# First group's value products taken pair by pair into four open banks, and router products placed between the steps of the maxima

## The chip, the cores and the metric

The kernel runs on one core of one Trainium2 chip. A core has TensorE (matrix products, PE in the profile), VectorE (DVE), ScalarE (ACT), GpSimd (POOL) and SyncE (SP, which here only issues DMAs), and 16 DMA engines that serve the queues of SP, ScalarE and GpSimd. Engines run side by side and wait for one another by semaphores; each works through its own queue in order. The metric is the device time of one execution in microseconds (us); lower is better. All data are 32-bit floats.

## The reference

`x` is 4096 x 512, the context `ctxt` is 3202 x 512. The first half of the layer is a gated attention of the rows of `x` over the context:

```python
encoder_hc = layernorm(x)                       # 4096 x 512
Sim  = (encoder_hc @ w1)[:, None] + (ctxt @ w2)[None, :] + (encoder_hc * w3) @ ctxt.T + b
A    = softmax(Sim, axis=context)
hq   = A @ ctxt                                 # the "values" product
Batt = softmax(max(Sim, axis=context), axis=rows)
hc   = Batt @ encoder_hc
hcq  = concat([encoder_hc, hq, encoder_hc * hq, encoder_hc * hc]) @ W_qv + b_qv
x    = x + tanh(g_xattn) * hcq
```

The second half is a mixture of 8 experts with 2 choices per row: router logits `layernorm(x) @ w_router`, capacity 640 rows per expert, `gelu(rows @ w1 + b1) @ w2 + b2`, and a gated sum back into the rows.

## The kernel before

**Tiling.** The 4096 rows are worked in 8 groups of 512. The context is cut into two halves of 12 tiles of 128 rows; tile j of both halves makes a pair (`NJ` = 12 pairs), and one tile of 128 and two single rows are left over. `PAIRS` joins two pairs at a time, so a group's score stage has six steps. Most products are done in Strassen's manner: seven products of quarter blocks in place of eight, with sums of the blocks formed on VectorE.

**Stages of a group g.** `stage_s(g)` makes the scores: in each of the six steps seven products (`pas`, `p6s`, `p7s`, `pbs`, `pas` again, `p4s`, `pbs` again; L507), each of eight TensorE instructions, and VectorE's sums of them (L467 to L481), of which L474 reads `pbs` between its two products; then the scores of the left-over tile (`sc`, L531), running maxima `M` (L525), a transposition (`mps`, L546), a reduction, and a product that spreads the maxima along rows (`mbps`, L159). `stage_d(g - 1)` makes the output products of the group before (L820). `stage_e(g)` subtracts the maxima on VectorE (L579) and takes exponentials on ScalarE (L580); VectorE sums them (L588). `stage_v(g)` makes the values product (`product`, L639). In it `between()` prepares the queries of the next group (`stage_w`, `stage_a` with L343 to L348 and the sums L189 to L192), and `early()` loads them. `stage_n(g)` reads rows of a later group for their means and variances and for single columns (L312 to L323, L183). At the end of `stage_v`, the two left-over context rows are added (L734), row sums (`rsps`, L738) give the scale `ri`, and the left operand of the output products is formed (L750 to L768).

**The first group is different.** It builds for the later groups what they only load. `build` forms the sums of the transposed context (`ktb`) and stores them (`kt_d`, L515). In `stage_v(0)` the values are not in Strassen's manner: in four passes (two column halves of 256, and in each the two context halves), value tiles of 6 x 128 x 256 are loaded by `load_values` (L442, L448) and multiplied into two open banks. Beside that, VectorE builds the sums of the values (`build_values`, L387 to L390), from row tiles that `rows_of_pair` loads separately (L380), into tiles `vs` with two buffers, which GpSimd's queue stores in `vs_d` (L391). It also builds the weights of the output products from `W_qv` (`build_weights`, L411 to L423), stored in `wt_d`. `router_weights` loads all of `W_qv` transposed (`wq`, L281), and 64 small products (L289, 8 columns wide) multiply it with the router's weights; one goes behind each value product (`beside`). Their result is copied to `we` (L664, L678, L679), which `build_weights` needs.

**What sets the order.** The program is traced once; a scheduler orders each engine's queue by program order among what it takes to be ready, with its own idea of durations. `tc.issue_after(ins)` puts what its block traces on the engine of `ins` behind `ins` in that queue. The list `queue` holds loads on SP's queue, and `queue[-1]` the latest of them. Tiles of one tag share buffers: tag `st` has five (keys, value tiles, output weights), `vs` two, `vc` two. There are six PSUM banks for products (`bank`) and two for transpositions (`ps_tr`).

Of the kernel before, what the change touches and what calls it, by code (L numbers as in the profile page):

```python
# [20 lines left out]
def gated_layer(ctx, tc, x, x_t, ctxt, ctxt_t, ctxt_c, ctxt_r, g_xattn, g_ffn, w_sim, w_sim_r, b_sim, W_qv, W_qv_t, b_qv, b_qv_c, w_router, b_router, w1, b1, w2, b2, out):  # L21
# [102 lines left out]
    with ExitStack() as s1:  # L124
# [141 lines left out]
        def router_weights():  # L266
# [16 lines left out]
            def products(ps, ks):  # L283

                for k in ks:
                    for a, f0, n in parts[k]:
                        for f in range(n // P):
                            for d in range(DC):
                                nc.tensor.matmul(  # L289
# [4 lines left out]
                                yield  # L294
# [3 lines left out]
        def we_bank(name):  # L298
            return bank(name).rearrange("p a b -> p (a b)")[:, : 4 * DC * E].rearrange("p (k c e) -> p k c e", k=4, c=DC)
# [76 lines left out]
        def rows_of_pair(j, name):  # L376
            vc = sb.tile([P, 2, D], F32, name=f"vc{name}{j}", tag="vc", bufs=2)
            for h in range(2):
                with tc.issue_after(queue[-1].ins):
                    nc.sync.dma_start(vc[:, h, :], ctxt[h * LH + j * P : h * LH + j * P + P, :])  # L380
            return vc

        def left_sums(name, vc, dst):
# [6 lines left out]
            tt(vs[:, 3, :], A12, vs[:, 1, :], ALU.subtract)  # L390
            nc.gpsimd.dma_start(dst, vs)  # L391

        def build_values(j):

            left_sums(f"v{j}", rows_of_pair(j, "v"), vs_d[j // JH][:, :, j % JH, :])

        def build_rest_values():
            vc = sb.tile([P, 2, D], F32, name="vcr", tag="vc", bufs=2)[:, 0, :]
            with tc.issue_after(queue[-1].ins):
                nc.sync.dma_start(vc, ctxt[LC : LC + P, :])  # L400
            vd = sb.tile([P, 256], F32, name="vd", tag="vs", bufs=2)
            tt(vd, vc[:, :256], vc[:, 256:], ALU.subtract)
            nc.gpsimd.dma_start(vd_d, vd)
# [79 lines left out]
        def stage_s(g):  # L483
# [8 lines left out]
            for jj, js in enumerate(PAIRS):  # L492
# [23 lines left out]
                if g == 0 and jj == 2:  # L516
                    with tc.issue_after(e_add.ins):
                        stage_a_rest(first_qs)
                if jj == 4 and 0 < g < NG - 1:
                    ahead[g + 1] = stage_n(g + 1)  # L520
# [7 lines left out]
            for i, terms in enumerate((((0, "1"), (1, "2")), ((2, "3"), (3, "7")))):  # L528
                for a, p in terms:
                    for k in range(2):  # L530
                        nc.tensor.matmul(  # L531
# [9 lines left out]
            tt(M[:, :, 0, :], M[:, :, 0, :], ec, ALU.max)  # L541
            if g == 0:
                live[g]["we"] = router_weights()
            ps = ps_tr.tile([P, 4, P], F32, name=f"mps{g}", tag="tr")
            for i in range(4):
                tr = nc.tensor.transpose(ps[:, i, :], M[:, i // 2, 0, (i % 2) * P : (i % 2 + 1) * P], ident)  # L546
# [4 lines left out]
            diag_rows(ps, f"m{g}", mt)  # L551
# [17 lines left out]
        def stage_e(g, first):  # L569
# [26 lines left out]
            if first:  # L596
                for h in range(2):
                    for jj in range(n_jj):
# [25 lines left out]
        def stage_v(g, early, between):  # L624
# [8 lines left out]
            def product(ps, what, right, start=True, stop=True, rest=None, right_c=None, beside=iter(())):  # L633
                for i in range(2):
                    vt = load_values(g, what, i, rest)
                    js = list(range(i * JH, (i + 1) * JH)) + ([NJ] if i and rest is not None else [])
                    for j in js:
                        for b in range(2):
                            mm = nc.tensor.matmul(  # L639
                                ps[b], vt[:, j - i * JH, b * P : (b + 1) * P], right(j) if j < NJ else right_c,  # L640
                                start=start and j == 0 and (b == 0 or g == 0), stop=stop and i == 1 and j == js[-1],
                                skip_group_check=True,
                            )
                            with tc.issue_after(mm.ins):
                                next(beside, None)
                return mm

            if g == 0:
                ps12, ps03 = we_bank("we12"), we_bank("we03")
                w12, w03 = v["we"](ps12, [1, 2]), v["we"](ps03, [0, 3])  # L650
                for i in range(2):
                    ps = [bank(f"vv{i}_{b}") for b in range(2)]
                    for h in range(2):
                        product(
                            ps, (h, i * 256), lambda j: E[j // 2][:, :, h, j % 2, :], start=h == 0, stop=h == 1,
                            rest=rest_of(i * 256) if h else None, right_c=ec, beside=w03 if i else w12,
                        )
                        if (i, h) == (0, 0):
# [839 lines left out]
```

## Time and profile before

| | |
|---|---|
| median of 3 runs | 2675.95 us (2674.36 to 2680.94) |
| the profiled execution's own time | 2675.19 us |
| its span in the trace | 2673.4 us |
| mean granted clock of TensorE | 0.988 |
| first group's `sc`, start in the trace | 90.56 us |
| first value product (`vv`) | 102.09 us |
| `rsps` of the first group | 204.64 us |
| second group's `sc`, start | 305.66 us |

The span is what the trace covers; the execution's own time is 1.8 us longer. Times inside the span count from its start. Two TensorE records make one 32-bit product. "L474" is line 474 of the kernel before. An arrow in brackets names what ended an idle stretch.

### The profile page before, as it was taken

What the parts mean: (1) busy time and instruction counts of PE and PEld (TensorE: products, weight loads), DVE (VectorE), ACT (ScalarE), POOL (GpSimd) and SP (SyncE); (2) the same over time, 40 slices, a digit from 0 to 9 for tenths busy, and PEclk for the clock granted to TensorE, in tenths of its full rate; (3) what the DMA queues carried; (4) which work ended last, traced back from release to release, by engine and by line L of the source; (5) the groups of instructions that cost most, each with busy time, mean ns of one, the idle gap of its engine ahead of it and who ended that gap; (6) DMA issues with size and microseconds to landing.
All of it is one profiled execution on the core that took longest, in us unless ns stands there. A gap on an engine that the chain in (4) does not pass through costs nothing. (4 is left out here: it accounts for less than half of the span.)

```text
span 2673.4 us, 29708 instructions
## 1 busy us (share of the span) xinstructions
PE 2593.4 (97%) x11200; PEld 2096.8 (78%) x11200; DVE 1706.4 (64%) x3432; ACT 458.4 (17%) x788; POOL 241.7 (9%) x301
## 2 busy tenths in 40 slices
PE   8996999999999999999999996999999999999998
PEld 7655888888888888888888875777777777777776
DVE  7854766856947768569466556574747575565654
ACT  1200110200201102002011143211121211111111
POOL 0110000100000001000000056000101010101010
PEclk9998999999999999999999997999999999999999
DMA  7776674756746747567446694322313242323210
GB/s 274 253 237 220 178 250 172 198 196 184 243 153 177 252 162 201 204 178 240 162 146 208 230 357 148 131 107 89 123 67 126 76 145 83 107 87 103 75 60 20
DMA packets 185007, 442.62 MB, mean 166 GB/s; under 512 B 17806, under 2 KB 84750, under 8 KB 182816
## 3 DMA queue, kind: packets, MB, share of 16 engines
q1 hardware_dynamic: 156960, 358.81, 41.1%
q0 software_dynamic: 17872, 51.46, 5.6%
q10 hardware_dynamic: 10032, 30.46, 2.9%
q8 instruction: 88, 1.44, 0.2%
q14 instruction: 55, 0.45, 0.1%
HBM read 362.27 MB, written 85.55 MB: 168 GB/s over the span
## 5 line engine op out<-in xcount | busy, mean ns | idle before, releaser
L507 PE MATMUL pas<-Qp,kt 128*128 128x256 f32 x672 | 161.6, 382 | 0.0
L1246 PE MATMUL pah<-bT,w 128*128 128x320 f32 x512 | 159.3, 434 | 0.5 <-ACT p1h L1253 0.5
L639 PE MATMUL pbv<-E,vt 128*128 128x256 f32 x672 | 147.3, 379 | 0.0
L507 PEld LDWEIGHTS pas<-Qp,kt 128*128 128x128 f32 x672 | 128.0, 191 | 17.4
L639 PEld LDWEIGHTS pbv<-E,vt 128*128 128x128 f32 x672 | 127.7, 190 | 17.4
L1246 PEld LDWEIGHTS pah<-bT,w 128*128 128x128 f32 x512 | 97.5, 191 | 39.8 <-ACT p1h L1253 1.0
L580 ACT ACTIVATE E<-E 128x1024 f32<-128x1024 f32 x96 | 100.9, 1057 | 129.5 <-DVE E L579 128.6
L579 DVE TENSOR_TENSOR E<-E,mb 128x1024 f32<-128x1024 f32 x96 | 115.3, 1216 | 11.4 <-ACT mb L566 11.4
L1246 PE MATMUL pao<-w,h 128*128 128x256 f32 x512 | 120.9, 379 | 0.0
L1429 POOL DMA_INDIRECT out<-acc,ti x40 | 40.9, 1022 | 863.0 <-DVE dc L1295 529.0
L1017 PE MATMUL x1p<-W,q2T 128*128 128x264 f32 x512 | 117.4, 390 | 0.0
L1406 PE MATMUL op<-w,h 128*128 128x512 f32 x256 | 114.8, 592 | 0.0
L1246 PEld LDWEIGHTS pao<-w,h 128*128 128x128 f32 x512 | 97.3, 190 | 20.1 <-issue 7.7
L1017 PEld LDWEIGHTS x1p<-W,q2T 128*128 128x128 f32 x512 | 97.7, 192 | 16.5
L463 ACT COPY p1s<-pas 128x512 f32<-128x512 f32 x48 | 28.1, 586 | 464.5 <-issue 257.2
L507 PE MATMUL pbs<-Qp,kt 128*128 128x256 f32 x336 | 81.3, 386 | 21.4 <-DVE E L474 21.4
L525 DVE TENSOR_TENSOR M<-M,E 128x1024 f32<-128x1024 f32 x80 | 97.9, 1224 | 4.5
L507 PEld LDWEIGHTS pbs<-Qp,kt 128*128 128x128 f32 x336 | 64.8, 193 | 30.8 <-DVE E L474 21.8
L1406 PEld LDWEIGHTS op<-w,h 128*128 128x128 f32 x256 | 46.6, 190 | 48.7 <-issue 41.4
L507 PE MATMUL pbs<-q,kt 128*128 128x256 f32 x336 | 79.4, 379 | 2.9 <-DVE we L679 2.9
L479 DVE TENSOR_TENSOR E<-p4s,u3s 128x512 f32<-128x512 f32 x48 | 33.1, 689 | 75.4 <-PE p4s L507 75.4
L1368 DVE TENSOR_TENSOR h<-p4h,u3h 128x320 f32<-128x320 f32 x64 | 31.3, 489 | 78.1 <-PE p4h L1246 78.1
(467 smaller groups left out, 5423.1 us busy)
## 6 DMA issues: line engine op xcount, KB each, us to landing
kt<-kt_d SPq DMA_DIRECT2D x84, 896.0 KB
w<-in_w SPq DMA_DIRECT2D x32, 2048.0 KB
vt<-vs_d SPq DMA_DIRECT2D x56, 768.0 KB
wp<-wt_d SPq DMA_DIRECT2D x56, 520.0 KB
kt_d<-ktb ACTq DMA_DIRECT2D x12, 896.0 KB
buf_d<-zero SPq DMA_DIRECT2D x80, 129.0 KB
xb<-buf_d SPq DMA_DIRECT2D x40, 258.0 KB
r<-r_d SPq DMA_DIRECT2D x32, 260.0 KB
```

The source lines that it names most:

```text
L463: nc.scalar.copy(p1, pa)
L479: tt(done(1, 0), p4, u3, ALU.add)
L507: nc.tensor.matmul(ps[:, jl, :], kts[j][:, KSLOT[p], k, :], B[p][:, k, :], start=start and jl == 0 and k == 0, stop=stop and k == 1, skip_ ...
L525: tt(M, M, e[:, :, h], ALU.max)
L579: live[g]["last"] = tt(e, e, m, ALU.subtract)
L580: live[g]["exp"] = nc.scalar.activation(e, e, AF.Exp)
L639: mm = nc.tensor.matmul(ps[b], vt[:, j - i * JH, b * P : (b + 1) * P], right(j) if j < NJ else right_c, start=start and j == 0 and (b == 0 ...
L1017: mm = nc.tensor.matmul(ps[:, j, :B1], qTs[g][:, c, q * P : (q + 1) * P], W1[:, c, j, :], start=(c == 0), stop=(c == DC - 1))
L1246: nc.tensor.matmul(ps, a, b, start=start and i == 0, stop=stop and i == len(A) - 1, skip_group_check=True)
L1368: tt(hi[:, :HC], ps, u, ALU.add)
L1406: nc.tensor.matmul(ps, hT[:, k, 2 * MH :], W2[:, k, :], start=(k == 0), stop=(k == KH - 1))
L1429: sc = nc.gpsimd.indirect_dma_start(out=out[:, :], out_offset=rows_of(ti, s), in_=acc[:, :], in_offset=None, bounds_check=N - 1, oob_is_er ...
```

## The change

1. *Values of the first group.* One pass over the pairs in place of four. `rows_of_pair(j)` loads both tiles of pair j in one DMA of 512 KB into a buffer of tag `st`, the loads being members of `queue`. TensorE takes the left operands of four products per tile from it, into four open banks, and VectorE's sums of the values read the same buffer. The separate value loads go. The scaled queries of the second group come behind the sums of the ninth pair (`sums`).
2. *Exponentials of the first group* are taken step by step with both context halves, in place of one half after the other.
3. *Router products.* The weights are loaded from the fourth step of the first group's scores on. All 64 products go into one bank, in a fixed order: 12 behind `sc`, 12 behind the transposition, 24 behind `mbps`, and one behind each of the first 16 value products, those of the first two pairs.
4. *Moved into the second group's scores:* behind the last sum (`e_add`) of step 0 the rest rows and `rsps` (`rest_rows`), behind that of step 1 the left operand (`left_operand`), and behind those of steps 1 to 4 one `build_weights` each. In the other groups `rest_rows` and `left_operand` stay at the end of `stage_v`.

```diff
+        def behind(mm, products, n):
+            for _ in range(n):
+                with tc.issue_after(mm.ins):
+                    mm = next(products, mm)
+            return mm
...
+        def rows_of_pair(j):
+            vc = st.tile([P, 2, D], F32, name=f"vc{j}", tag="st")
+            with tc.issue_after(queue[-1].ins):
+                if j < NJ:
+                    rows = ctxt[:LC, :].rearrange("(h j p) d -> p h j d", h=2, p=P)[:, :, j, :]
+                    queue.append(nc.sync.dma_start(vc, rows))
+                else:
+                    queue.append(nc.sync.dma_start(vc[:, 0, :], ctxt[LC : LC + P, :]))
             return vc
...
                 if g == 0 and jj == 2:
                     with tc.issue_after(e_add.ins):
                         stage_a_rest(first_qs)
+                if g == 0 and jj == 3:
+                    live[g]["we"] = router_weights()
+                if g == 1:
+                    with tc.issue_after(e_add.ins):
+                        if live["then"]:
+                            live["then"].pop(0)()
+                        if 0 < jj <= DC:
+                            build_weights(jj - 1)
...
-            if g == 0:
-                live[g]["we"] = router_weights()
+                beside = live[g]["we"](pw, [1, 2, 0, 3])
+            mm = behind(mm, beside, 12)
             ps = ps_tr.tile([P, 4, P], F32, name=f"mps{g}", tag="tr")
             for i in range(4):
-                tr = nc.tensor.transpose(ps[:, i, :], M[:, i // 2, 0, (i % 2) * P : (i % 2 + 1) * P], ident)
+                with tc.issue_after(mm.ins):
+                    mm = nc.tensor.transpose(ps[:, i, :], M[:, i // 2, 0, (i % 2) * P : (i % 2 + 1) * P], ident)
+            mm = behind(mm, beside, 12)
...
-            diag_rows(ps, f"m{g}", mt)
+            with tc.issue_after(mm.ins):
+                mm = diag_rows(ps, f"m{g}", mt)
+            live[g]["beside"], live[g]["mm"] = beside, behind(mm, beside, 24)
...
-                for h in range(2):
-                    for jj in range(n_jj):
+                for jj in range(n_jj):
+                    for h in range(2):
                         powers(E_t[jj][:, :, h], mb.unsqueeze(2).to_broadcast([P, 2, 2, 256]))
...
+                ps = [bank(f"vv{b}") for b in range(DC)]
+                for j in range(NJ + 1):
+                    vc = rows_of_pair(j)
+                    for h in range(2 if j < NJ else 1):
+                        for b in range(DC):
+                            with tc.issue_after(mm.ins):
+                                mm = nc.tensor.matmul(
+                                    ps[b], vc[:, h, b * P : (b + 1) * P], E[j // 2][:, :, h, j % 2, :] if j < NJ else ec,
+                                    start=j == 0 and h == 0, stop=j == NJ, skip_group_check=True,
+                                )
+                            mm = behind(mm, beside, 1)
+                    with tc.issue_after(v["last"].ins):
+                        if j < NJ:
+                            total = build_values(j, vc)
+                        else:
+                            build_rest_values(vc[:, 0, :])
+                    if j == 2:
+                        with tc.issue_after(v["last"].ins):
+                            nc.vector.tensor_copy(we, v["pw"])
+                    if j == 3:
+                        with tc.issue_after(v["last"].ins):
+                            ahead[1] = stage_n(1)
+                    if j == 5:
+                        early()
+                    if j == 8:
+                        v["sums"] = total
+                for b in range(DC):
+                    nc.scalar.copy(hqT[:, b, :], ps[b].rearrange("p a b -> p (a b)"))
                 between()
...
+            if g:
+                rest_rows()
+                left_operand()
+            else:
+                live["then"] = [rest_rows, left_operand]
...
-                    stage_a(g + 1, live.pop("qT"), ahead[g + 1][0], live[g]["last"], live[g]["exp"])
+                    stage_a(g + 1, live.pop("qT"), ahead[g + 1][0], live[g].get("sums", live[g]["last"]), live[g]["exp"])
```

## The prediction

> **What bounds the kernel now.** First the page's busy times: TensorE is busy nearly throughout, so a change pays only where TensorE waits, works twice or works cold.
>
> ```profile
> PE 2593.4 (97%) x11200; PEld 2096.8 (78%) x11200; DVE 1706.4 (64%) x3432; ACT 458.4 (17%) x788; POOL 241.7 (9%) x301
> ```
>
> Second, the waits of TensorE from 0 to 260 us (us in total, times, longest). Nearly all the idle time that the diff can reach is one wait of 21.4 us at the second group's start.
>
> ```profile
> PE pbs L507 <- DVE E L474: 23.3, 3, 21.4
> ...
> PE vv L639 <- ACT E L580: 3.0, 1, 3.0
> PE pbs L507 <- DVE we L679: 2.9, 1, 2.9
> PE mbps L159 <- DVE dgm L158: 1.7, 1, 1.7
> PE mps L546 <- DVE M L541: 1.4, 1, 1.4
> ```
>
> Third, TensorE's timeline: start, length, instruction, idle before. A value product and a router product take 1.09 together (112.00 to 113.09), a value product alone 0.858 (24 instructions, two to a product, in 10.30, 142.56 to 152.86): the router's adds 0.22.
>
> ```profile
> 90.56 3.62 PE L531 MATMUL sc<-Qp,kcb 128*128 128x256 f32 x16
> ...
> 102.09 2.07 PE L639 MATMUL vv<-E,vt_(0_0)_0_821 128*128 128x512 f32 x2 [3.02 <-ACT E L580]
> ...
> 112.00 1.10 PE L639 MATMUL vv<-E,vt_(0_0)_0_821 128*128 128x512 f32 x2
> 112.95 0.28 PE L289 MATMUL we<-wrc,wq 128*128 128x8 f32 x2
> 113.09 1.10 PE L639 MATMUL vv<-E,vt_(0_0)_0_821 128*128 128x512 f32 x2
> ...
> 142.56 10.46 PE L639 MATMUL vv<-E,vt_(1_0)_1_977 128*128 128x512 f32 x24
> ...
> 204.64 0.95 PE L738 MATMUL rsps<-ones,mb 128*128 128x1 f32 x8
> ...
> 240.99 3.78 PE L507 MATMUL pbs<-Qp,kt 128*128 128x256 f32 x8 [21.38 <-DVE E L474]
> ```
>
> Fourth, VectorE's timeline just before 241. It stands still for store landings between the last sums, then takes the first group's rest rows and left operand, and only at 240.24 the sum that frees TensorE's bank. So it is VectorE's order, not its load, that stops TensorE.
>
> ```profile
> 225.01 0.42 DVE L402 TENSOR_TENSOR vd<-vcr 128x256 f32<-128x256 f32 x1 [2.82 <-DMA vs_d<-vsv]
> 228.49 0.43 DVE L419 TENSOR_TENSOR wt<-wc 128x260 f32<-128x260 f32 x1 [3.06 <-DMA vs_d<-vsv]
> ...
> 230.01 0.74 DVE L734 SCALAR_TENSOR_TENSOR hqT<-prb,cr,hqT 128x512 f32<-128x512 f32 x1
> ...
> 240.24 0.69 DVE L474 TENSOR_TENSOR E<-pbs,u3s 128x512 f32<-128x512 f32 x1
> ```
>
> **The change part by part.** Against the profiled execution's 2675.19 us, 0.8 below the median.
>
> *Stall removed.* Rest rows, left operand and right-hand weights go behind steps 0 to 4 of the second group's scores. 2.88 + 21.38 = 24.3 go. After the stall 14 matmuls took 5.97 (240.99 to 246.96) where the next eight took 1.72, 0.216 each: 14 x 0.216 = 3.0, so 2.9 of half clock go too.
>
> *Router products.* The stretch from the end of `sc` (94.18) to 204.64 is 110.5 now. After: 48 of the 64 products stand before the values. Alone, eight such small matmuls took 0.81 (204.64 to 205.45), so a product of two costs 0.20: 48 x 0.20 = 9.6, transposes 0.7, column product 0.9. Values start at 94.2 + 11.2 = 105.4, which is 3.3 later than now, since 9.6 of work goes into 6.1 of waits (1.4 + 1.7 + 3.0) and the order is strict: transposes and column product stand behind their 12 products even when their data is ready. Then 100 value products x 0.858 = 85.8 and 16 router products x 0.22 = 3.5: end 194.7. Gain 204.6 - 194.7 = 9.9, which includes 2.3 of half-clock start. `rsps` (0.8) only moves. Four bank copies of 0.59 on ScalarE now follow the last value where two did; the second group's third product is the first to need one of these banks, 3.5 in, so 0.
>
> *Their weights,* eight loads of 512 KB on SP's queue, are issued from the fourth step of the first group's scores on. A window query gives a DMA share of 0.00 for 60 to 65, and SP waits there for a key buffer, so I take 0; if they came as late as now (issued until 89.9, used at 103), the maxima would wait up to 9.
>
> *Rows shared.* Thirteen row loads replace ten value loads and 25 row loads; 6.4 MB less traffic. TensorE takes 8 x 0.858 = 6.9 per pair (8.6 in the first two); five buffers let loading run 34 us ahead. What is new is that a buffer is freed only when VectorE's four sums (4 x 0.34 = 1.4) are done too. VectorE's queue in this phase: 15 of subtraction, 15 of column sums, 13 of `stage_n`, 19 of sums, 10 of query work and pooling: 72 in the 95 from 100 to 195. I take 0: the lead of 34 hides it, and rival 3 is what it costs without that cover. Two waits are added on VectorE. The copy of the router weights needs the 64th product, at 105.4 + 16 x 1.08 = 123; VectorE is busy with column sums until then, and the sums of values behind the copy have their lead: 0. The query work of the second group now stands behind the ninth pair's sums, at about 160, and takes some 10 with ScalarE's four scalings; ScalarE and then TensorE's second group wait for it, and that group starts at 195: 25 to spare. The new order of the exponentials delivers two pairs per 2.3 against a use of 13.8: 0.
>
> *Work moved.* Rest rows 8 x 0.66 + 4 x 0.61 + 0.9 = 8.6; left operand 4 x 1.14 + 4 x 0.61 + 0.1 = 7.1; weights 1.5 each. A step of the scores is 7 x 1.727 = 12.1 on TensorE with 5.7 on VectorE. The last of a step's seven products goes into `pbs` again and so needs E (L474) done 10.4 after the step's start, while the moved work enters behind the last add of the step before. In step 1: that add 0.7, rest rows 8.6, one maximum 1.1, then u2, u3 and E 1.9: 12.3, about 2 too many; step 2, with left operand and first weights (8.6 again), the same. Later steps get 1.5 more each, the last of them beside the 11 of `stage_n` that it has now without a stall. A new stall of 4.2, between 0 (if the planner interleaves as at 60 to 80 us, with VectorE full and 0.2 lost) and 10. On SP's queue the key loads stand behind the weight loads; they run a step ahead (12), and a landing costs 3 to 6, so 0. GpSimd gets eight weight stores, and the last two decide when the first group's output products start: VectorE is done about 68 after the group's start, issue 0.8, landing 5.5 (a store issued until 222.98 released VectorE at 228.49), weight load 3: 77, against keys 72.5, stall 4.2 and `sc` 3.5: 80. Cost 0, with a margin of 3; without it, rival 1.
>
> **Two rules against it.** GpSimd's rows under a busy VectorE:
>
> ```profile
> 107.73 6.41 POOL L563 TENSOR_SCALAR nl<-lmax 128x1 f32<-128x1 f32 x1 [9.00 <-issue]
> ...
> 164.57 0.71 POOL L391 DMA_DIRECT2D vs_d<-vsv  x1 [9.77 <-DVE vsv L390]
> ```
>
> The first took 6.41 while VectorE ran its subtractions without a gap (the same instruction of the second group, among sums from PSUM, took 0.36 at 321.48); the store issue took 0.71 though VectorE ran gapless there too. The Trainium skill ("SBUF — State Buffer", "SBUF: two separate sides") says that VectorE and GpSimd share a port pair held by one of them for a whole instruction, and that GpSimd's DMA descriptors can be starved so. By the rule the stores lose up to the 8.6 of rest rows, output products start 5 late: 2648. By the store's row, nothing. I take the row, which is of the same kind of instruction.
>
> ```profile
> 98.00:100.00 2.00, 1.07 (x2) 0.24 (x2) 0.49 (x4) 0.59 (x1) 0.38 (x1) 1.00 1.07 388
> 100.00:102.00 2.00, 0.00 (x0) 0.00 (x0) 2.00 (x2) 1.02 (x1) 0.00 (x0) 0.50 1.04 383
> ```
>
> These are two rows of TensorE's windows; after the busy times come PEclk, the granted clock, then DMA share and GB/s. TensorE worked 1.07 of 2 and then nothing, and the clock was half from 100 until 107. The skill ("TensorE: Matmul & The Clock Gate", "What's actually happening") has the clock halved after an idle window of about 3.4 us and restored after a busy one. It does not say whether eight-column products count as busy. If not, the last 24 cost 0.40 each (+4.8) and the values start cold (+2.3): 7.1 worse. I take full clock, because with the products TensorE has no idle stretch left between 94 and 105; both ends are in the range.
>
> **Sum.** 24.3 + 2.9 + 9.9 = 37.1, less 4.2: 32.9. 2675.2 - 32.9 = 2642.3; on the median 2643.
>
> **Rivals.**
> 1. The work moved stops the second group (0.21): GpSimd's queue is in order, and `stage_n` of the third group waits there for a landing (12.0 at L322 in this group now); weight stores behind it start the output products some 9 late, or VectorE waits inside the steps for store landings as now (3.1 each). Against: the weights come first in the program. 2643 + 10 = 2653.
> 2. Small products run cold or their weights land late (0.08): 2650.
> 3. Slower (0.05): the shared rows tie TensorE to VectorE's sums, which wait for GpSimd's stores through two `vs` buffers. From before, sums came 6 to 9 us apart with DMA near full, once 20. It decides from about 11 a pair: nine pairs from 118 give 217, query work 10, second group at 227, the gain gone. At 12.5: 240, 13 late: about 2689. Against: DMA is freer and the lead is five tiles.
> 4. Nothing (0.02): the planner leaves the same landings ahead of E (L474), one stall for the other.
>
> **How the numbers follow.** Forecast 0.64, with 2637 to 2650 (stall 0 to 10). Over rivals 1 and 2 the range is 2634 to 2658; the slower case is left out. 0.3%, 8 us, is about what a measurement tells from no change: faster 0.93, same 0.02, slower 0.05.
>
> **What would show it.** Right: `rsps` late inside the second group's keys; values from 105 to 195; no TensorE wait over 4 us before 270; the second group's `sc` near 272 (305.66 now); clock 1.00 from 94 to 110. Wrong: TensorE waiting for row loads at `vv`, for `wp` at L820, or long again at `pbs`.

## The result and the profile after

The changed kernel takes 2651.24 us (median of 4 runs, 2649.48 to 2653.13), beside 2676.84 for the kernel before in the same session. The ratio is 0.9903, 95% interval 0.9886 to 0.992. The profiled execution's span is 2649.1 us, 24.3 less than before. The forecast was 2643.0 with a range of 2634 to 2658.

The page's busy times, after. TensorE is busy 5.0 us longer than before (2598.4 against 2593.4), and its idle time fell from 80.0 to 50.7; the difference is the 24.3 us.

```profile
PE 2598.4 (98%) x11200; PEld 2101.7 (79%) x11200; DVE 1703.0 (64%) x3430; ACT 458.6 (17%) x788; POOL 234.6 (9%) x301
```

The waits of TensorE from 90 to 330 us, after (us in total, times, longest). The 21.4 and the 2.9 at `pbs` are gone, and so are the three around the maxima (1.4, 1.7 and 3.0). A new one stands at the output products (L850, which was L820).

```profile
PE pad L850 <- DMA wp<-wt_d: 4.1, 1, 4.1
PE pbs L512 <- DVE E L479: 0.3, 1, 0.3
```

TensorE's timeline after (start, length, instruction, idle before in brackets). L289 is a router product, L677 a value product of the first group, L544 `sc`, L662 the values of the second group.

```profile
90.94 3.62 PE L544 MATMUL sc<-Qp,kcb 128*128 128x256 f32 x16
94.39 2.74 PE L289 MATMUL we<-wrc,wq 128*128 128x8 f32 x24
...
97.46 3.18 PE L289 MATMUL we<-wrc,wq 128*128 128x8 f32 x24
100.49 2.05 PE L159 MATMUL mbps<-dgm,ones 128*128 128x512 f32 x2
102.34 10.25 PE L289 MATMUL we<-wrc,wq 128*128 128x8 f32 x48
112.44 2.06 PE L677 MATMUL vv<-E,vc 128*128 128x512 f32 x2
...
131.82 68.91 PE L677 MATMUL vv<-E,vc 128*128 128x512 f32 x160
200.57 3.60 PE L677 MATMUL vv<-Ec,vc 128*128 128x512 f32 x8
...
216.09 0.95 PE L759 MATMUL rsps<-ones,mb 128*128 128x1 f32 x8
...
278.29 3.62 PE L544 MATMUL sc<-Qp,kc 128*128 128x256 f32 x16
286.05 2.56 PE L850 MATMUL pad<-wp,hqT 128*128 128x260 f32 x8 [4.14 <-DMA wp<-wt_d]
```

The values end at 204.0, hardly earlier than before (204.64). They start at 112.44 where 105.4 was forecast: the last 24 router products took 10.25, 0.43 each instead of 0.20. From there to `sc` the second group takes 74.3; before it took 101.0.

VectorE's timeline at the seam, after. The last sum of the first group's rows is done at 192. VectorE then waits for TensorE, not the other way round, and the rest rows (L755) come behind the first step's sums.

```profile
191.64 0.42 DVE L407 TENSOR_TENSOR vd<-vc 128x256 f32<-128x256 f32 x1
207.73 0.69 DVE L472 TENSOR_TENSOR u2s<-p6s,p1s 128x512 f32<-128x512 f32 x1 [15.67 <-PE p6s L512]
...
211.11 0.69 DVE L479 TENSOR_TENSOR E<-pbs,u3s 128x512 f32<-128x512 f32 x1 [1.04 <-PE pbs L512]
...
216.90 5.38 DVE L755 SCALAR_TENSOR_TENSOR hqT<-prb,cr,hqT 128x512 f32<-128x512 f32 x8
```

An account by four marks of TensorE's timeline, each stretch beside the same one before:

| stretch | before | after | gained | forecast |
|---|---|---|---|---|
| start to end of the first group's values | 204.64 | 204.01 | 0.6 | 9.9 |
| from there to the second group's `sc` | 101.0 | 74.3 | 26.7 | 23.0 (24.3 + 2.9 - 4.2) |
| `sc` to the second group's values (`pav`) | 29.5 | 35.4 | -5.8 | 0 |
| from there to the end | 2338.2 | 2335.5 | 2.8 | 0 |
| sum | | | 24.3 | 32.9 |

So the total is within the forecast's range although every term is off, and that is in part luck: 15.1 us of gain that did not come (9.3 and 5.8) stand against 6.5 that came unforecast (3.7 and 2.8). The experiments take the terms in turn.

### The profile page after: what moved, and what is told of

It reads as the page before. It is cut to its first block, busy times and chain, and to the rows that moved or that the text cites. A ratio compares the mean times of both kernels' runs of the same rounds, so it can differ in the third digit from the quotient of the medians.

```text
span 2649.1 us, 29673 instructions
## 1 busy us (share of the span) xinstructions
PE 2598.4 (98%) x11200; PEld 2101.7 (79%) x11200; DVE 1703.0 (64%) x3430; ACT 458.6 (17%) x788; POOL 234.6 (9%) x301
## 2 busy tenths in 40 slices
DMA packets 178255, 436.06 MB, mean 165 GB/s; under 512 B 17454, under 2 KB 77998, under 8 KB 176064
## 5 line engine op out<-in xcount | busy, mean ns | idle before, releaser
L662 PE MATMUL pbv<-E,vt 128*128 128x256 f32 x672 | 147.3, 379 | 0.0
L662 PEld LDWEIGHTS pbv<-E,vt 128*128 128x128 f32 x672 | 127.7, 190 | 17.3
L677 PE MATMUL vv<-E,vc 128*128 128x512 f32 x192 | 88.2, 610 | 0.0
L481 ACT COPY E<-pas 128x512 f32<-128x512 f32 x48 | 28.1, 585 | 306.5 <-PE pas L512 296.7
L1276 PE MATMUL p6h<-x,w1s 128*128 128x320 f32 x256 | 80.2, 436 | 0.0
```

The lines of the kernel that those rows point to most:

```text
L662: nc.tensor.matmul(ps[b], vt[:, j - i * JH, b * P : (b + 1) * P], right(j) if j < NJ else right_c, start=start and j == 0 and b == 0, stop ...
L677: mm = nc.tensor.matmul(ps[b], vc[:, h, b * P : (b + 1) * P], E[j // 2][:, :, h, j % 2, :] if j < NJ else ec, start=j == 0 and h == 0, sto ...
L1276: nc.tensor.matmul(ps, a, b, start=start and i == 0, stop=stop and i == len(A) - 1, skip_group_check=True)
```

## The experiments

Each kernel was run beside the kernel before on the same chip; the times differ a little from session to session, so ratios are compared. "V2" is the start of the second group's first value product in the trace (before 335.2, after 313.7). It is less disturbed by what happens later than the total is: from V2 to the end the kernels took 2334.6 to 2342.4.

| kernel | median, us | ratio to before, 95% interval | V2 |
|---|---|---|---|
| changed kernel | 2651.2 | 0.9903 (0.9886 to 0.992) | 313.7 |
| e1_beside | 2652.2 | 0.9912 (0.9895 to 0.9928) | 316.1 |
| e2_wide | 2650.6 | 0.9907 (0.9891 to 0.9924) | 312.4 |
| e3_stage_n_later | 2660.8 | 0.9947 (0.993 to 0.9963) | 315.9 |
| e4_rest_back | 2657.6 | 0.9931 (0.9914 to 0.9947) | 316.6 |
| e5_weights_back | 2650.4 | 0.9906 (0.9888 to 0.9924) | 309.6 |
| e6_mixed | 2646.5 | 0.9897 (0.9881 to 0.9914) | 306.9 |
| e7_rows_twice | 2652.7 | 0.9916 (0.9896 to 0.9935) | 314.9 |
| e8_weights_early | 2652.0 | 0.9918 (0.9901 to 0.9934) | 309.9 |
| e9_mr_queue | 2655.8 | 0.9938 (0.9922 to 0.9955) | 313.5 |
| e11_mix_weights | 2647.9 | 0.9895 (0.9876 to 0.9913) | 309.1 |
| e12_vector_old | 2673.6 | 0.9997 (0.9986 to 1.0009) | 334.7 |
| e13_row_sums_old | 2652.8 | 0.9919 (0.99 to 0.9938) | 312.8 |

### Where did the router products' gain go: the clock

The windows of TensorE after (window, its length, busy time and count of PE, PEld, DVE, ACT, POOL, then granted clock, DMA share, GB/s). TensorE is busy 2.00 of 2 in every row, and from 100 on the clock is half. In the kernel before it was also half here, from 100 to 107, but there TensorE had been idle from 94 on for most of the time.

```profile
98.00:100.00 2.00, 2.00 (x18) 2.00 (x18) 1.53 (x6) 0.00 (x0) 0.26 (x1) 0.90 0.55 204
100.00:102.00 2.00, 2.00 (x5) 1.30 (x6) 0.00 (x0) 0.00 (x0) 0.12 (x1) 0.50 0.01 3
...
110.00:112.00 2.00, 2.00 (x11) 2.00 (x11) 2.00 (x3) 2.00 (x5) 1.33 (x1) 0.50 0.00 0
...
118.00:120.00 2.00, 2.00 (x9) 1.04 (x8) 2.00 (x3) 0.53 (x2) 0.00 (x0) 1.00 0.00 0
```

**e1_beside**: no product in the waits; all 64 behind value products.

```diff
-            mm = behind(mm, beside, 12)     # behind sc, and again behind the transposition
+            mm = behind(mm, beside, 0)
...
-            live[g]["beside"], live[g]["mm"] = beside, behind(mm, beside, 24)
+            live[g]["beside"], live[g]["mm"] = beside, behind(mm, beside, 0)
...
-                    if j == 2:
+                    if j == 7:
                         with tc.issue_after(v["last"].ins):
                             nc.vector.tensor_copy(we, v["pw"])
```

> All 64 router products stand beside the first 64 value products again; the waits for the maxima are empty. Theory (the clock halves from about 100 us whatever small products stand there, so the 48 moved products earned nothing): value products start at about 102.5 instead of 112.4, run at half clock at first, carry 64 x 0.22 and end at about 204.8 against 204.0: 2650 to 2653, within 2 us of the changed kernel's 2651. Rival (the moved products do earn the forecast 10 us, and the changed kernel lost them elsewhere, for instance by rows shared between TensorE and VectorE): values end near 214, 2661.

The values end at 205.8, 1.8 later than after; the ratio cannot be told from the changed kernel's. TensorE is idle in the waits again (1.40, 1.71 and 3.02), starts the values at 102.33 and gets the full clock back at 109, where the changed kernel gets it at 117. The 48 products that the change moves save 0.22 each beside the values, 10.6 together, but the values start 10.1 later (112.44 instead of 102.33), and that gives it back.

**e2_wide**: as e1, and in the three waits 2, 2 and 4 products of 512 columns whose result nobody reads.

```diff
+            def wide(mm, n):
+                for i in range(n if g == 0 else 0):
+                    with tc.issue_after(mm.ins):
+                        mm = nc.tensor.matmul(fill, ident, live[0]["qT"][:, i % DC, :], start=True, stop=True)
+                return mm
...
-            mm = behind(mm, beside, 12)
+            mm = wide(mm, 2)                # then again 2, and 4 in place of 24
```

> Like the run with all router products beside the values, but 2, 2 and 4 products of 512 columns whose result nobody reads stand in the three waits for the maxima. Theory (the clock follows how much the array streams, not whether TensorE has an instruction): granted clock 1.00 from 94 us into the values, which start at about 102.8 without a slow start and end at 202.8: 1.2 us before the changed kernel, about 2650. Rival (the clock falls at about 100 for a reason that work on TensorE does not touch): 0.50 from 100, the last fillers take 1.7 each, values start after 106 and end after 206, 2653 to 2655.

The same stretch is now filled with wide products, and the clock stays at 1.00 (windows of e2_wide):

```profile
98.00:102.00 4.00, 4.00 (x10) 1.67 (x10) 2.49 (x5) 1.64 (x2) 0.38 (x1) 1.00 0.01 5
102.00:106.00 4.00, 4.00 (x15) 2.26 (x15) 4.00 (x4) 3.74 (x4) 0.34 (x1) 1.00 0.00 0
```

The values start at 102.25 and end at 202.4. So it is not the idle time but what runs that decides: both kernels show TensorE without a gap, one with eight columns to a product and one with 512.

**e6_mixed**: in the waits four router products and one wide one in turns (one, one and two such blocks); the other 48 behind value products.

```diff
+            def mixed(mm, n):
+                for _ in range(n if g == 0 else 0):
+                    mm = wide(behind(mm, beside, 4), 1)
+                return mm
...
-            mm = behind(mm, beside, 12)
+            mm = mixed(mm, 1)               # then again 1, and 2 in place of 24
```

> In the waits for the maxima stand blocks of four router products and one product of 512 columns whose result nobody reads: one block, one and two; the other 48 router products go beside the first 48 value products. Theory (what keeps the clock is the share of time in which columns stream): if half the time is enough, the clock stays 1.00, values start at 102.3 and end at 198.9, 5 us before the changed kernel: about 2646. Rival (any stretch of small products lowers it): 0.50 from about 100, values end after 203, 2650 or more.

TensorE's timeline of e6_mixed. A block of four small products takes 0.81 (eight instructions, next start less this one), the wide one 0.94, and the values start at 102.68.

```profile
99.17 0.95 PE L289 MATMUL we<-wrc,wq 128*128 128x8 f32 x8
99.98 1.10 PE L567 MATMUL fill<-qT,ident 128*128 128x512 f32 x2
100.92 0.95 PE L289 MATMUL we<-wrc,wq 128*128 128x8 f32 x8
...
102.68 1.02 PE L689 MATMUL vv<-E,vc 128*128 128x512 f32 x2
```

And a window of it, at the place where the changed kernel has 0.50:

```profile
100.00:102.00 2.00, 2.00 (x13) 1.52 (x13) 2.00 (x2) 0.75 (x1) 0.00 (x0) 1.00 0.00 0
```

With about half of the time in wide products the clock stays full. The values end at 199.2, 4.8 before the changed kernel's; V2 is 6.8 earlier and the span 5.2 shorter (2643.9). That is the lowest median of all runs, and this kernel computes the whole layer; but the interval of its ratio overlaps the changed kernel's, so the times alone do not show a gain over it: it rests on one trace of each.

### What removed the wait of 21 us

The forecast said that VectorE's order made it, and gave the gain to the moved rest rows, left operand and weights. Here the parts are put back, alone and together.

**e4_rest_back**: rest rows and left operand again at the end of the first group's values.

```diff
-                live["then"] = [rest_rows, left_operand]
+                live["then"] = []
+                rest_rows()
+                left_operand()
```

> Rest rows and left operand stand at the end of the first group's values again; the weights stay in the second group's scores. Theory (VectorE's order at the seam makes the stall): 15.7 us of work stand before u2, u3 and E of the second group, which TensorE needs 10.4 after the group's start at 204: E at about 224, a wait of 9 to 10 at pbs and 2 to 3 of half clock after it, 2661 to 2664. Rival (store landings made the old stall, and these are gone): a wait under 3, 2650 to 2654.

The stall of 9 to 10 did not come. Rest rows begin at 203.2, as soon as the last values are copied, and the sum that frees TensorE's bank (L479) at 217.11; TensorE had taken the next step's `pas` and two instructions of its `p6s` ahead of the `pbs` that needs it, and waited for nothing here: its only wait from 90 to 330 is at the output products. (The 1.1 us that two later expectations name for this place is a wait in the first group's scores, before 90.) What was lost sits later. The weights' stores now came behind a wait in GpSimd's queue; GpSimd's timeline of e4_rest_back:

```profile
278.72 0.59 POOL L325 DMA_DIRECT2D mrb<-mr_d  x1 [9.84 <-DMA buf_d<-zero]
279.31 0.78 POOL L421 DMA_DIRECT2D wt_d<-wc  x1
280.08 0.76 POOL L428 DMA_DIRECT2D wt_d<-wt  x1
```

and the output products waited 6.9 for them. This is the place that rival 1 of the forecast named, though here it was called up by putting the other work back.

**e5_weights_back**: weights again among the first group's values, behind the sums of pairs 5, 7, 9 and 11.

```diff
-                        if 0 < jj <= DC:
-                            build_weights(jj - 1)
...
+                    if j in (5, 7, 9, 11):
+                        with tc.issue_after(v["last"].ins):
+                            build_weights((j - 5) // 2)
```

> The four weight blocks (build_weights) are built among the first group's values again, behind the sums of pairs 5, 7, 9 and 11; rest rows and left operand stay in the second group's scores. The run with rest rows back had shown that these cost only 1.1 us at the seam. Theory (the old stall was VectorE's backlog of sums and weights, whose tiles go through two vs buffers and wait some 5 us each for GpSimd's stores to land): four more tiles put the last one near 212 instead of 191.6, E of the second group near 214 against a need at 214.4: a wait of 0 to 4 at pbs, and no wait for wp at the output products: 2645 to 2651. Rival (weights alone made the stall): a wait of 10 to 20 at pbs, 2662 or more.

TensorE waits 1.1 at `pbs`, and not at all at the output products; V2 is 4.0 earlier than after. The total is the same within its interval.

**e7_rows_twice**: VectorE loads its rows of the context a second time, through two buffers of its own.

```diff
+        def rows_again(j):
+            vc = sb.tile([P, 2, D], F32, name=f"vcv{j}", tag="vc", bufs=2)
...
-                            total = build_values(j, vc)
+                            total = build_values(j, rows_again(j))
...
-                            build_rest_values(vc[:, 0, :])
+                            build_rest_values(rows_again(j)[:, 0, :])
```

> VectorE loads its rows of the context a second time, through two slots of its own, as in the kernel before; all else as after. My theory (sharing the rows is worth nothing in time: the sums of the first group's pairs are finished at 191 us after the change, 12 us before the second group's keys begin, and the loads are 6.4 MB of traffic in 100 us): within 2 us of the changed kernel's gain, 23 to 27 us under the kernel before, no TensorE wait over 1 us at the second group's pbs, the third group's values start within 2 us of 313.65. Rival (the two slots were what held VectorE's sums back in the kernel before): the sums end after 204 us, TensorE waits 3 to 10 us at pbs of the second group, and 3 to 10 us of the gain are gone.

The waits are about the changed kernel's (3.7 at the output products, 0.4 at `pbs`); V2 is 1.2 later. Sharing the rows is worth 6.6 MB of traffic (442.62 against 436.06) and nothing in time that this measurement can tell. The last sums were done at 203.5, where the changed kernel has 192, and that was still in time.

**e13_row_sums_old**: the row sums as before: loaded again, in four batches of three pairs, the second group's query work not tied to the ninth pair.

```diff
+                        if j in (2, 5, 8, NJ):
+                            for i in range(j // 3 * 3 - 3 * (j == NJ), j // 3 * 3 + 3 * (j < NJ)):
+                                total = build_values(i, rows_again(i))
+                            if j == NJ:
+                                build_rest_values(rows_again(NJ)[:, 0, :])
...
-                    if j == 8:
-                        v["sums"] = total
```

> Only the row sums are put back as before (rows loaded again, four batches, query work ahead of the batches); weights, rest rows and left operand stay inside the second group's keys as after. Theory A1 (the row sums alone carry most of the backlog: each batch waits for the landings of its own stores, 3 to 5 us at a time): TensorE waits 6 to 15 us at the second group's first pbs and 6 to 15 us of the gain are gone. Theory A2 (it takes row sums, weights and rest rows together to reach past the 36 us of cover that the keys' products give): a wait under 4 us at pbs, time within 4 us of the changed kernel's gain.

**e12_vector_old**: the same, and in each batch the weights of before, with rest rows and left operand at the end of the values. TensorE's side stays that of the changed kernel.

```diff
-                        if 0 < jj <= DC:
-                            build_weights(jj - 1)
...
+                            for c in [[], [0, 1], [2], [3]][j // 3 - j // NJ]:
+                                build_weights(c)
...
-                live["then"] = [rest_rows, left_operand]
+                live["then"] = []
+                rest_rows()
+                left_operand()
```

> TensorE's order stays as after (pair by pair into four banks, router products in the wait for maxima), but VectorE's side is put back as before: rows loaded again, sums in four batches of three pairs with the second group's query work ahead of the batch of pairs 4 to 6 on, weights behind the batches, rest rows and left operand at the end of the values. Theory A (the old stall of 21 us was VectorE's backlog, whatever TensorE's order): TensorE waits 12 to 22 us at the second group's first pbs, the second group's sc starts at 291 to 301, and only 2 to 12 us under the kernel before are left. Theory B (the old stall came with TensorE's order in four passes): a wait under 5 us at pbs, time 14 to 22 us under the kernel before.

TensorE's waits from 90 to 330, first e13_row_sums_old:

```profile
PE pad L859 <- DMA wp<-wt_d: 3.1, 1, 3.1
PE pas L522 <- DMA kt<-kt_d: 0.8, 1, 0.8
PE pbs L522 <- DVE E L489: 0.3, 1, 0.3
```

and e12_vector_old:

```profile
PE pas L522 <- DMA kt<-kt_d: 12.3, 2, 6.6
PE pbs L522 <- DVE E L489: 5.0, 1, 5.0
PE p6s L522 <- DVE u2s L482: 2.6, 1, 2.6
```

With all of VectorE's work back in its old place the whole gain is gone (0.9997, interval 0.9986 to 1.0009), although TensorE keeps its new order and its router products in the waits. With the row sums alone back, nothing is lost at `pbs`, though the last of them is done only at 206: what the forecast moved is by itself enough to remove the wait. So the old wait was the backlog of three things, and each of them, put back alone, fits beside the values and the first products of the keys. VectorE's timeline of e12_vector_old shows the chain: each remaining sum waits for rows or for the landing of a store (two buffers each), then come weights and rest rows, and only at 242.45 the sum for TensorE.

```profile
216.95 0.42 DVE L404 TENSOR_TENSOR vsv<-vcv 128x256 f32<-128x256 f32 x1 [7.19 <-DMA vcv<-in_ctxt]
...
226.94 0.43 DVE L434 TENSOR_TENSOR wt<-wc 128x260 f32<-128x260 f32 x1 [3.27 <-DMA vs_d<-vsv]
228.55 5.51 DVE L764 SCALAR_TENSOR_TENSOR hqT<-prb,cr,hqT 128x512 f32<-128x512 f32 x8
...
242.45 0.69 DVE L489 TENSOR_TENSOR E<-pbs,u3s 128x512 f32<-128x512 f32 x1
```

The form differs in one point from before, where all 21.4 stood at `pbs`. Here most of it stands at `pas`: SP's queue of e12_vector_old issues the keys behind row loads that wait for VectorE's buffers.

```profile
202.35 1.39 SPq L442 DMA_DIRECT2D kt<-kt_d  x1
211.50 0.92 SPq L395 DMA_DIRECT2D vcv<-in_ctxt  x2
212.50 0.42 SPq L442 DMA_DIRECT2D kt<-kt_d  x1
```

Pairs of the three parts were not tried, so it stays open how the 21 us divide among them, and whether the earlier row sums would have been enough with everything else in its old place.

### The new wait before the output products

In the forecast this had a margin of 3 us. In the changed kernel the first load of the output weights is issued at 273.80, as soon as its store has landed, and lands 12.1 later, where loads of this kind took 5.1 in the median. In that time the DMA engines move little, in most windows while they count as busy (windows of after):

```profile
274.00:276.00 2.00, 2.00 (x11) 1.74 (x11) 1.90 (x3) 0.58 (x1) 0.34 (x1) 1.00 1.08 17
276.00:278.00 2.00, 2.00 (x10) 1.57 (x9) 1.75 (x3) 0.00 (x0) 0.00 (x0) 1.00 0.08 6
278.00:280.00 2.00, 2.00 (x11) 1.76 (x10) 1.90 (x3) 0.00 (x0) 0.00 (x0) 1.00 1.09 56
```

Just before, GpSimd issues a store of single numbers, the row statistics of the third group (`mr_d`, L324), and one of weights. From the DMA issues of after, 262 to 290 us (KB, median us to landing); the six stores of weights before these two took 3.4 to 8.3:

```profile
wt_d<-wc POOLq DMA_DIRECT2D x1, 520.0 KB, 4.6
wt_d<-wt POOLq DMA_DIRECT2D x1, 520.0 KB, 13.9
...
mr_d<-mr POOLq DMA_DIRECT2D x1, 4.0 KB, 9.8
```

**e3_stage_n_later**: the third group's row statistics one step later.

```diff
-                if jj == 4 and 0 < g < NG - 1:
+                if jj == (5 if g == 1 else 4) and 0 < g < NG - 1:
```

> In the second group alone, the reading of the third group's rows (stage_n) comes one step of the scores later, so its store of 1024 single numbers (mr_d) is issued after the last weight store and not before it. Theory (the last weight store took 13.9 us to land because it stood behind those single numbers in GpSimd's DMA queue): the store lands in about 5, TensorE does not wait for wp, and its output products start at full clock: 5.6 us less, 2645 to 2646. Rival (the weights are simply built too late, or the DMA engines are full of the zeros stored at that time): the wait of 4 us at the first output product stays, 2650 to 2652.

The output products wait for nothing, but VectorE now stands 7.0 for the rows that the statistics read, ahead of the sum that frees TensorE's bank, and TensorE with it:

```profile
267.69 0.69 DVE L317 BATCH_NORM_STATS2 st<-q 128x6 f32<-128x512 f32 x1 [7.02 <-DMA q<-in_x]
```

TensorE waits 4.5 at `pbs` and goes on at half clock; V2 is 2.3 later than after. The wait was traded for another. (The ratio, 0.9947, is worse than the changed kernel's by more than V2 explains; the rest is not explained.)

**e8_weights_early**: e4, and the weights one step earlier, in steps 0 to 3.

```diff
-                        if 0 < jj <= DC:
-                            build_weights(jj - 1)
+                        if jj < DC:
+                            build_weights(jj)
```

> Rest rows and left operand at the end of the first group's values (1.1 us of stall when run alone), and the four weight blocks behind steps 0 to 3 of the second group's scores instead of 1 to 4. Theory (the last weight store lands late because it meets mr_d and the wait of mrb on GpSimd's queue): it is issued some 12 us earlier, ahead of both; no wait for wp, output products at 282, the second group's values at 308 against 313.7: 2645 to 2646. Rival (the DMA engines are full with keys and zeros then, whenever the store is issued): a wait of 3 or more for wp stays, 2650.

No wait at the output products, V2 at 309.9. A wait of 2.7 at `pbs` came in the fourth step, where VectorE stands 5.0 for the same load of rows (`q`); the median is that of the changed kernel.

**e9_mr_queue**: the store of single numbers issued by ScalarE instead of GpSimd, for the third group only.

```diff
-            nc.gpsimd.dma_start(mr_d[g].rearrange("k i p -> p k i"), mr)
+            (nc.scalar if g == 2 else nc.gpsimd).dma_start(mr_d[g].rearrange("k i p -> p k i"), mr)
```

> The store of single numbers mr_d of the third group goes through ScalarE's DMA queue; all else as in the changed kernel. Theory (order within one queue: the last weight store stood behind 1024 single numbers in GpSimd's): it lands in about 5 instead of 13.9, no wait for wp, 5 to 6 less: 2645 to 2647. Rival (the single numbers or the zeros occupy the DMA engines, whatever queue they come from): it still takes over 9, the wait for wp stays at 3 to 4, 2650 to 2652.

The wait is 2.7 instead of 4.1, GpSimd still stands 10.1 for the landing of that store, and the slow stretch remains. So it does not come from the order within GpSimd's queue. (The ratio, 0.9938, is worse than the changed kernel's, V2 is not; what was lost after V2 is not explained.) e3 and e8 show that the wait goes when the weights land away from the statistics.

Both the 4 KB store and the 520 KB one are under way in that stretch of the changed kernel. In e5_weights_back the last weights were stored some 50 us before, and still GpSimd stands 9.1 for the small store while little is moved, with loads of weights under way (GpSimd's timeline, then windows, of e5_weights_back):

```profile
265.03 1.01 POOL L324 DMA_DIRECT2D mr_d<-mr  x1 [0.30 <-POOL mr L322]
275.78 0.58 POOL L325 DMA_DIRECT2D mrb<-mr_d  x1 [9.10 <-DMA mr_d<-mr]
```

```profile
268.00:270.00 2.00, 2.00 (x11) 1.75 (x10) 1.89 (x3) 0.05 (x1) 0.00 (x0) 1.00 0.66 19
270.00:272.00 2.00, 2.00 (x11) 1.77 (x10) 1.42 (x2) 0.53 (x1) 0.00 (x0) 1.00 0.91 58
```

So the stretch does not need the large store. The kernel before has one too (10 to 48 GB/s from 294 to 302, small store issued at 290.68), and so do the changed kernel's first values (4 to 18 GB/s from 158 to 164, small store issued at 154.36), where VectorE stood 10.2 for a store of sums. What all of them share is the small store just ahead. No run leaves it out, so that it makes the others slow is the likeliest reading and not shown.

### Both improvements together

**e11_mix_weights**: e6 and e5 in one kernel.

```diff
+                    mm = wide(behind(mm, beside, 4), 1)
...
+                    if j in (5, 7, 9, 11):
+                        with tc.issue_after(v["last"].ins):
+                            build_weights((j - 5) // 2)
```

> Two parts of earlier runs together: four router products and one wide product that nobody reads, in turns, in the wait for the maxima (keeps the clock at 1.00), and the first group's weights among its own values instead of in the second group's keys (no wait for the last weight store). Theory (the two gains sit at different places and add): values of the first group end near 199, no wait at the output products, the third group's values start at 301 to 304, time 2641 to 2645, 30 to 34 us under the kernel before. Rival (the stretch after the third group's values gives back 3 to 5 us, as with the weights moved alone): third group's values at 301 to 304 but time 2645 to 2649.

They do not add. The values end 5.9 earlier than in e5 (199.2 against 205.1), but VectorE's work beside them has not become shorter: its last weight sums wait until 207.21 for a store, and L479 is done at 212.8. TensorE waits 3.2 and starts again at half clock; V2 is 309.1, where 301 to 304 was expected.

```profile
207.21 0.43 DVE L424 TENSOR_TENSOR wt<-wc 128x260 f32<-128x260 f32 x1 [6.25 <-DMA vs_d<-vsv]
...
210.54 0.68 DVE L472 TENSOR_TENSOR u2s<-p6s,p1s 128x512 f32<-128x512 f32 x1
...
212.13 0.69 DVE L479 TENSOR_TENSOR E<-pbs,u3s 128x512 f32<-128x512 f32 x1
```

## Why the prediction was right, step by step

*Stall removed* (24.3 and 2.9 of half clock): held, and the reason given with it too. The stretch shortened by 26.7, e12_vector_old shows that VectorE's order carries practically the whole result, and e13_row_sums_old, which keeps the moved rest rows, left operand and weights and gives up the earlier row sums, keeps the gain. What the forecast did not see is that it moved more than was needed, because the row sums (done at 192 instead of 225 and costed at nothing) are part of the same backlog: e4 put back rest rows and left operand, e5 the weights, e13 the row sums, and each waited 1.1 or less at `pbs`. Of the combinations tried, only all three together make the wait.

*Router products* (9.9): this step failed. 0.6 was measured, because the choice of full clock was wrong; that TensorE had no idle stretch left was right, but it did not keep the clock. The other end was in the text: 7.1 worse. Measured: 24 products 10.25 against 4.8 (5.4), the second 12 0.8 more, the column product 1.0 more, and the first two value records at 2.05 where 1.1 is full (1.9), together 9.1. The Trainium skill ("TensorE: Matmul & The Clock Gate", "What's actually happening") says that the clock follows how busy TensorE has been recently; here the profile's busy column, 2.00 of 2 at half clock, is no measure of that. Rival 2 named this price, with a chance that was too low. That its time, 2650, is nearly the measured 2651 is luck, since the other terms were off as well and happened to cancel.

*Their weights* (0): held; the eight loads are issued from 53.0 to 65.0 and nothing waits for them.

*Rows shared* (0): held in time, by e7. The single steps slipped without effect: the copy of the router weights is at 136.3 instead of 123, because the 64th product is later by the lost clock (131.7) and VectorE was then busy with other sums; the query work starts at 176 instead of 160, mainly because VectorE waited 10.2 for a store of sums. TensorE never waited for rows, so rival 3 did not come; nor did rival 4, one stall for the other at L474.

*Work moved* (-4.2): too dear. Of the new stall in steps 1 and 2 nothing was seen. The rest rows went behind the first step's sums as forecast, but the scheduler put the second step's sums (L472 to L479) between them and the left operand; after 206 no wait of TensorE over 0.4 is in the keys. The forecast's lower bound, 0, was the right end.

*Last weight store, margin 3* (0): the second mis-sized term. Ready 81.9 after the group's start instead of 77, since the load put at 3 took 12.1; needed at 77.9 instead of 80, since the stall of 4.2 did not come. The wait is 4.1, and the output products ran cold behind it (2.56 and 2.65 for eight, 1.92 before), so that the stretch took 5.8 more. The store's landing was no longer than forecast (4.6 for 5.5); the load met the slow stretch behind the store of single numbers. This is rival 1's place, at less than half its price of 10. Its counter-argument, that the weights come first in the program, failed for the last of them: that store was issued at 273.56, behind the statistics' at 272.38.

*The rule of the shared port:* the row was the better guide. The stores of weights in the second group's keys were issued in 0.75 to 0.78 with VectorE nearly gapless. The forecast had also taken the rule too widely: the Trainium skill, in the section that it cites ("SBUF — State Buffer", "SBUF: two separate sides"), ties the starved descriptors to VectorE instructions in a two-port mode, and no trace here shows that VectorE was in one.

*The rest of the kernel* gave 2.8 that nobody forecast. It varies by several us among these kernels, mostly in short waits of the dispatch (`pos`); no cause is claimed.

The forecast came out 8 us too low: the products and the output products brought 9.3 and 5.8 less than hoped, the stall and the rest of the kernel 3.7 and 2.8 more.

## What to carry to other kernels

A long wait behind an engine that works in order is a backlog against a cover: once the backlog is below the cover, taking more away brings nothing, and a part put back alone costs nothing. So a single undo can't divide such a gain; put everything back first, and then each part, alone and in pairs.

A wait filled with small matrix products is not filled for the clock. Look at the granted clock in windows, not at the busy share, and where independent small products are to be used as filling, set wide ones between them (e6_mixed: V2 6.8 earlier, the total not told apart from the changed kernel's).

## What the runs showed of the hardware

- In the changed kernel TensorE, gapless with products of 8 columns but for four transposes and one 512-column product among them, fell to half clock within about 5 us of the first (94.4; 0.90 in the window 98 to 100), stayed there for 17 us, and recovered after about 4 us of 512-column products (112.4 to 117). Four of 8 columns and one of 512 in turns kept it at 1.00.
- DMA engines at a share near 1 moved only 17 and 56 GB/s in two windows of the changed kernel: while a 4 KB store of single numbers was under way (9.8 to landing), a 520 KB store took 13.9, where the seven others took 3.4 to 8.3, and a 520 KB load 12.1, where 5.1 was the median. The same slow stretch followed that small store with no large store under way (e5_weights_back).
